# Layer 0 of a four-layer convolution stack: depthwise taps in halves three taps apart, with expansions on the free rows

## The chip, the cores and the metric

The kernel runs on one core of one Trainium2 chip. A time is the device time of one execution in microseconds. The core has TensorE (matrix products, "PE" in the profile, with its weight loads as "PEld"), VectorE (DVE), ScalarE (ACT), GpSimd (POOL) and SyncE (SP, which here only issues transfers). TensorE multiplies a stationary block of up to 128x128 with moving columns, and can be used as smaller tiles: a product with 32 rows and 32 columns takes one of 16 such tiles, one with 64 and 64 takes a quarter of the array. The rows of a tile are the partitions that its operands lie on, its columns are the partitions of the result in PSUM.

## The reference, cut to what matters

Four layers, each `x = x + layer(group_norm(x))`, on x of 4 images, 64 channels, 256x256, in fp32. Only layer 0 is touched:

```
def _L0_conv_ref(x, w_in, w_dw, fft_filter, w_out):
    x = einsum('bchw,oc->bohw', x, w_in)             # 64 -> 384 channels ("expansion")
    xf = rfft2(8x8 patches of x) * fft_filter        # a filter on each patch's spectrum
    x = irfft2(xf) put back together
    x = depthwise 3x3 convolution of x with w_dw, zero padding 1
    x1, x2 = split(x, 2, axis=1)                     # 192 and 192 channels
    x = gelu(x1) * x2
    return einsum('bchw,oc->bohw', x, w_out)         # 192 -> 64
def _gn(v, G=32, eps=1e-5):                          # mean and variance over 2 channels x H x W
    ...
```

Layer 1 is a dense 3x3 convolution, layer 2 a choice between two 1x1 convolutions by the local differences, layer 3 a product of the lowest Fourier modes.

## The kernel before, in words

An image is cut into 32 tiles of eight rows (NJ = 32), 128 tiles in all (NS). Layer 0 is a loop over steps t, with the parts of several tiles in one step: taps and gating of tile t, projection and residual of tile t - 1, expansion and inversion of tiles t + 1 and t + 2, and transposition and transformation of tile t + 2. The order of the instructions on TensorE, VectorE, ScalarE and SyncE is the order in which the program states them (`tc.manual_schedule`); semaphores make them wait for each other across engines. GpSimd runs in its own order.

For one tile: `normalize_x` (ScalarE) normalizes x. `transpose_x` (L358) makes eight 128x128 transpositions, so that the 64 pixels of a patch lie on partitions, two patches one above the other. `transform_x` (L366) multiplies with the patch transform in 64x64 tiles (L372). `expand` (L378, products at L385) multiplies spectra with w_in: 64 channels to 384, so each product has 64 rows, 64 columns of results and 384 moving elements. The four products of one call, two halves s of rows times two halves n of results, fill the array. VectorE then multiplies the two PSUM banks with the filter (L388) into `up`. `invert` (L415, products at L423, 64x64 with 64 moving elements) transforms back, and ScalarE copies the result into one of three planes y with a border (L430): plane 0 and 1 hold the first 128 of x1 and of x2, plane 2 the other 64 of both.

The depthwise convolution of planes 0 and 1 is done on TensorE, that of plane 2 on VectorE (`vector_tap`, nine instructions a tile, L488, the first on ScalarE, L486). On TensorE a tap is a product with a diagonal 32x32 block. `depthwise` (L442) goes through nine taps k, in each through four quarters q of the channels (rows of the array) and four chunks j of two image rows (columns of the array): 16 tiles of 32x32 with 512 moving elements (L450), into two pairs of PSUM banks, quarters 0 and 1 into the first, 2 and 3 into the second. A plane is done on all 16 tiles for nine taps; plane 0 gets a gelu on ScalarE (`gate_part`, L464), plane 1 is multiplied to it by VectorE (`value_part`, L470). `project` multiplies with w_out in 64x64 (L516) and 32x64 tiles (L525), `add_residual` and `finish` add x and take the statistics for layer 1. Transfers are tied to certain taps, so that they come at a set point of the step (`after`).

PSUM is four pairs of banks, given out in turn (`pair`). The statistics of image 0 come first: 32 parts of 8 rows, each loaded in two transfers to 64 partitions (L277), two VectorE instructions each (L269). A partition holds every second group of four rows of one channel. Those of the later images are taken in the steps, one part or two a step, `AHEAD` = 4 parts ahead (L570).

Of the kernel before, what the change touches and what calls it, by code (L numbers as in the profile page):

```python
# [17 lines left out]
C = 64  # L18
# [51 lines left out]
def _constants(H, W):  # L70
# [3 lines left out]
    avg = (grp[:, None] == grp[None, :]) / np.sum(grp == 0)  # L74
    half = np.arange(128) // C
# [9 lines left out]
        "c_ident": np.eye(128), "c_avg32": avg32, "c_sel32": sel32, "c_fdft": f_blk, "c_bdft": b_blk, "c_pick": pick, "c_avg": avg,  # L85
# [29 lines left out]
class _Net:  # L115
# [53 lines left out]
    def group_norm_parts(self, n, b, bst):  # L169


        nc, sp = self.nc, self.sp
# [4 lines left out]
        nc.tensor.matmul(ps[:, 0:1], self.avg, mv[:, 0:1], start=True, stop=True)  # L177
# [5 lines left out]
        nc.vector.scalar_tensor_tensor(q, d, d, mv[:, 1:2], ALU.mult, ALU.add)  # L183
        yield
        ps2 = self.small(f"gv{n}_{b}")
        nc.tensor.matmul(ps2[:, 0:1], self.avg, q, start=True, stop=True)
# [58 lines left out]
    def _layer0(self, ctx, dst):  # L245
# [3 lines left out]
        turn = count()  # L249

        def pair(name):

            return pp.tile([128, 2, 512], F32, tag=f"p{next(turn) % 4}", name=name)

        small = self.small = lambda name: pair(name)[:, 0, :]
# [9 lines left out]
        def input_stats(t, k, bst):  # L265
            tf = t.rearrange("p r w -> p (r w)")
            n = 4 * W // 512
            for i in range(n):
                nc.vector.bn_stats(bst[:, k * n + i, :], tf[:, i * 512 : (i + 1) * 512])  # L269

        new_bst0 = lambda b: self.sp.tile([128, NJ * 4 * W // 512, 6], F32, tag="bst0", name=f"bst0_{b}")
        with tc.tile_pool(name="l0i", bufs=12) as p_i:
            bst0 = new_bst0(0)
            for k in range(NJ):
                t = p_i.tile([128, 4, W], F32, tag="st", name=f"st_{k}")
                for s in range(2):
                    nc.sync.dma_start(t[halves[s]], src_t[0, :, k, s])  # L277
                input_stats(t, k, bst0)
            self.group_norm(0, 0, bst0)
# [78 lines left out]
        def transpose_x(t):  # L358
            xn = xns.pop(t)
            ps = pair(f"psT_{t}").rearrange("p z (k m) -> p (z k) m", m=128)  # L360
# [5 lines left out]
        def transform_x(t):  # L366
            x = xT.pop(t)
            ps = pair(f"psF_{t}").rearrange("p n (k m) -> p n k m", m=C)
# [9 lines left out]
        def expand(t, g, k):  # L378

            if k == 0:  # L380
                ups[t, g] = p_u.tile([128, 2, 4, 384], F32, tag="up", name=f"up_{t}_{g}")
            ps = pair(f"psu_{t}_{g}_{k}")
            for s in range(2):
                for n in range(2):
                    nc.tensor.matmul(  # L385
                        ps[halves[n], s, 0:384], xf[t][halves[s], n, 4 * g + k], win[halves[s]], start=True, stop=True
                    )
            nc.vector.tensor_mul(ups[t, g][:, :, k, :], ps[:, :, 0:384], flt.broadcast_to([128, 2, 384]))  # L388
# [26 lines left out]
        def invert(t, g, i):  # L415

            up = ups[t, g]
            ps = pair(f"psy_{t}_{g}_{i}").rearrange("p n (s r k w) -> p n s r k w", s=2, r=8, k=4)
# [23 lines left out]
        def depthwise(t, i, *transfers):  # L442


            d = [pair(f"psd_{t}_{i}_{m}").rearrange("p z (r w) -> p z r w", r=2) for m in range(2)]
            for k in range(9):
                dy, dx = divmod(k, 3)
                for q in range(4):
                    for j in chunks_of(t):
                        ins = nc.tensor.matmul(  # L450
                            d[q // 2][quarters[j], q % 2], diag[quarters[q], i, k, :],
                            rows_in(t, i, quarters[q], j, dy)[:, :, dx : dx + W],
                            start=(k == 0), stop=(k == 8), tile_position=(q * Q, j * Q),
                        )
                if k % 2 == 0 and k // 2 < len(transfers):
                    f, *args = transfers[k // 2]
                    f(*args, ins=ins)
            return d

        def gate_part(t, d):  # L460
            p = slice(0, Q * len(chunks_of(t)))
            h = ht[t] = p_h.tile([128, 4, 2, W], F32, tag="h", name=f"h_{t}")
            for m in range(2):
                nc.scalar.activation(h[p, 2 * m : 2 * m + 2], d[m][p], AF.Gelu)  # L464

        def value_part(t, d):
            p = slice(0, Q * len(chunks_of(t)))
            for m in range(2):
                hm = ht[t][p, 2 * m : 2 * m + 2]
                nc.vector.tensor_mul(hm, hm, d[m][p])  # L470
# [34 lines left out]
        def project(t, *groups):  # L505

            if 0 in groups:
                po[t] = [pair(f"pso_{t}_{m}") for m in range(1 if t == NS else 2)]
# [61 lines left out]
        AHEAD = 4  # L570

        def parts_of(t):
            if t < 0:
                return []
            more = [NJ + t // 6] if t < 6 * AHEAD and t % 6 == 4 else []
# [12 lines left out]
        def next_stats(t):  # L588
            for k in parts_of(t):
                b, j = place(k)  # L590
                if b not in bst0s:
                    bst0s[b], left[b] = new_bst0(b), NJ
                input_stats(st.pop(k), j, bst0s[b])
# [10 lines left out]
        with ordered:  # L604
# [3 lines left out]
            for t in range(2):  # L608
                normalize_x(t)
                transpose_x(t)  # L610
                transform_x(t)
            for k in range(4):
                expand(0, 0, k)
            new_y(0)
            for k in range(4):
                expand(0, 1, k)
                if k < 3:
                    invert(0, 0, k)
            for k in range(4):
                expand(1, 0, k)  # L620
                if k < 3:
                    invert(0, 1, k)
            vector_taps(0, 0)

            for t in range(NS + 2):

                if exists(t + 1):
                    new_y(t + 1)  # L630
                vector_gelu(t - 1, 0)
                normalize_x(t + 2)
                vector_taps(t, 1)
                vector_gate(t - 1, 0)
                vector_gelu(t - 1, 1)
                vector_taps(t, 2)
                vector_gate(t - 1, 1)
                vector_taps(t, 3, 4)
                if t <= NS:
                    loads = [(load_r, t, 0), (load_r, t, 1)]  # L640
                    if exists(t + 3):
                        loads += [(load_x, t + 3, 0), (load_x, t + 3, 1)]
                    gate_part(t, depthwise(t, 0, *loads))
                next_stats(t - 1)
                self.next_norms()

                if exists(t + 2):
                    transpose_x(t + 2)
                if exists(t + 1):
                    invert(t + 1, 0, 0)  # L650
                if t - 1 in rt:
                    project(t - 1, 0)
                if exists(t + 2):
                    transform_x(t + 2)
                if t - 1 in rt:
                    project(t - 1, 1, 2, 3)
                vector_taps(t, 5)
                if t - 1 in rt:
                    add_residual(t - 1)
                if exists(t + 1):  # L660
                    invert(t + 1, 0, 1)
                    expand(t + 1, 1, 0)
                    expand(t + 1, 1, 1)
                    invert(t + 1, 0, 2)
                    expand(t + 1, 1, 2)
                    expand(t + 1, 1, 3)
                if t - 1 in rt:
                    finish(t - 1)
                self.next_norms()

# [696 lines left out]
```

## Time and profile before

| | us |
|---|---|
| time, median of 3 runs (lowest to highest) | 7640.96 (7629.38 to 7649.89) |
| the profiled execution: time | 7615.35 |
| the profiled execution: span, first to last instruction | 7613.6 |
| PE busy | 7280.2 (96%) |
| DVE busy | 6592.5 (87%) |
| ACT busy | 3657.3 (48%) |
| L450, taps on TensorE | 2532.6 (73296 passes) |
| L488, taps on VectorE | 2390.8 |
| L385, expansions | 787.5 (8192 passes) |
| L423, inversions | 922.7 (49152 passes) |

"Busy" is the time in which at least one instruction of the group runs; matmuls overlap on TensorE, and their ends are modelled, so the starts carry more than the durations. A line of a group reads: line, engine, operation, result<-operands, tile of the array (rows*columns), shape of the moving operand, number. In an answer in order of time the first two numbers are the start and the length in us. An fp32 product appears as two matmul instructions, and each with its weight load. A row of a stretch gives the stretch, its length, and the busy time of PE, PEld, DVE, ACT and POOL with the number of instructions, then the clock granted to TensorE (1.00 is full speed), the busy share of the DMA engines and GB/s.

### The profile page before, as it was taken

The numbers are of one execution on the slowest core, as the hardware profiler recorded it, in microseconds if no ns is written. First come the engines' busy times: TensorE is split into PE (matmuls) and PEld (weight loads), VectorE is DVE, ScalarE is ACT, GpSimd is POOL, SyncE is SP. The second block draws the span as 40 slices with busy tenths as digits, with TensorE's granted clock in tenths as the row PEclk, the third lists the DMA queues.
The fourth block names the chain that finished last, engine by engine and source line by source line (L and its number), as shares of the span: only waits on it lengthen the run. The fifth ranks groups of instructions, "written<-read, shape, count | busy, mean of one in ns | idle before, by whom it ended". The sixth has DMA issues, their size and how long they took to land. (4 is left out here: it accounts for less than half of the span.)

```text
span 7613.6 us, 398948 instructions
## 1 busy us (share of the span) xinstructions
PE 7280.2 (96%) x189302; PEld 4316.7 (57%) x189302; DVE 6592.5 (87%) x5914; ACT 3657.3 (48%) x3917; POOL 658.8 (9%) x1435
## 2 busy tenths in 40 slices
PE   5999999999999999999999999899989999998797
PEld 3666666666666666666666666433324444443276
DVE  6999999999999999999999899899989888885345
ACT  2444444454544445444454454322238778774111
POOL 0000000000000000000000000001102222221011
PEclk9999999999999999999999999999999999999955
DMA  4222222222222222222111111478766766667789
GB/s 121 64 65 62 60 64 61 59 60 63 61 59 60 60 63 61 64 61 54 46 46 47 47 48 46 102 196 199 193 161 172 178 170 175 171 178 232 243 334 395
DMA packets 651427, 875.50 MB, mean 115 GB/s; under 512 B 44500, under 2 KB 470436, under 8 KB 647748
## 3 DMA queue, kind: packets, MB, share of 16 engines
q1 hardware_dynamic: 568772, 581.48, 29.0%
q0 software_dynamic: 81024, 268.50, 12.2%
q8 instruction: 1485, 24.33, 1.4%
q14 instruction: 146, 1.20, 0.1%
HBM read 581.37 MB, written 268.44 MB: 112 GB/s over the span
## 5 line engine op out<-in xcount | busy, mean ns | idle before, releaser
L450 PE MATMUL psd<-y,diag 32*32 32x512 f32 x73296 | 2532.6, 597 | 13.6 <-issue 13.0
L488 DVE SCALAR_TENSOR_TENSOR v<-y,sb_w_dw,v 128x2048 f32<-128x2048 f32 x1024 | 2390.8, 2335 | 110.7 <-ACT v L486 88.0
L450 PEld LDWEIGHTS psd<-y,diag 32*32 32x32 f32 x73296 | 1529.5, 103 | 851.3 <-issue 331.1
L430 ACT COPY y<-psy 128x512 f32<-128x512 f32 x1536 | 915.7, 660 | 1676.6 <-PE psy L423 1675.1
L388 DVE TENSOR_TENSOR up<-psu,flt 128x768 f32<-128x768 f32 x1024 | 932.5, 951 | 218.2 <-PE psu L385 217.7
L423 PEld LDWEIGHTS psy<-sb_c_bdft,up 64*64 64x64 f32 x49152 | 853.5, 135 | 345.0 <-issue 135.8
L423 PE MATMUL psy<-sb_c_bdft,up 64*64 64x64 f32 x49152 | 922.7, 221 | 27.3 <-issue 25.0
L385 PE MATMUL psu<-win,xf 64*64 64x384 f32 x8192 | 787.5, 489 | 22.2 <-DVE h L470 9.6
L988 DVE TENSOR_TENSOR q<-xn 128x2313 f32<-128x2313 f32 (+2 forms) x256 | 627.1, 2492 | 1.7 <-ACT xn L226 1.7
L1043 PE MATMUL one<-z,wp 32*32 32x512 f32 x16384 | 595.2, 598 | 19.6 <-issue 14.6
L989 ACT ACTIVATE q<-q 128x2313 f32<-128x2313 f32 (+2 forms) x256 | 528.9, 2086 | 33.4 <-DVE q L988 31.9
L226 ACT ACTIVATE xn<-x,nb,r 128x1024 f32<-128x1024 f32 (+3 forms) x272 | 488.0, 1798 | 42.2 <-DMA x<-x 32.3
L464 ACT ACTIVATE h<-psd 128x1024 f32<-128x1024 f32 x258 | 251.0, 1023 | 519.1 <-PE psd L450 518.8
L1043 PEld LDWEIGHTS one<-z,wp 32*32 32x32 f32 x16384 | 365.8, 103 | 227.9 <-issue 87.1
L1002 PE MATMUL div<-q,ones 64*32 64x512 f32 x8192 | 468.0, 597 | 12.3 <-ACT q L989 9.8
L395 POOL MEMSET y<- 128x22 f32 x384 | 51.9, 136 | 4228.6 <-ACT y L403 3219.8
L385 PEld LDWEIGHTS psu<-win,xf 64*64 64x64 f32 x8192 | 301.2, 134 | 191.5 <-issue 90.6
L1076 POOL DMA_DIRECT2D x<-r x512 | 273.6, 541 | 972.2 <-DVE r L1073 943.3
L797 PE MATMUL m<-t,wk 64*64 64x512 f32 x3072 | 352.7, 588 | 0.0
L797 PE MATMUL m<-t,wg 64*64 64x512 f32 x3072 | 343.6, 591 | 4.5 <-DVE wg L759 4.5
L1002 PEld LDWEIGHTS div<-q,ones 64*32 64x32 f32 x8192 | 156.1, 107 | 317.5 <-issue 246.0
L812 ACT COPY s<-m 128x1024 f32<-128x1024 f32 x64 | 64.8, 1013 | 558.9 <-PE m L797 548.7
(131 smaller groups left out, 7619.4 us busy)
## 6 DMA issues: line engine op xcount, KB each, us to landing
x<-x SPq DMA_DIRECT2D x240, 640.0 KB, 6.2
x<-x SPq DMA_DIRECT2D x122, 1024.0 KB, 11.6
st<-in_x_dram SPq DMA_DIRECT2D x256, 256.0 KB, 3.5
x<-in_x_dram SPq DMA_DIRECT2D x256, 256.0 KB, 3.8
x<-o POOLq DMA_DIRECT2D x128, 512.0 KB, 9.2
r<-x SPq DMA_DIRECT2D x512, 128.0 KB, 4.0
x<-r POOLq DMA_DIRECT2D x512, 128.0 KB, 3.9
out_dram<-x POOLq DMA_DIRECT2D x64, 1024.0 KB, 9.8
```

What stands on the lines that cost most here:

```text
L226: self.nc.scalar.activation(dst, src, AF.Identity, bias=self.nb[n][p0:p1, b : b + 1], scale=self.r[n][p0:p1, b : b + 1])
L385: nc.tensor.matmul(ps[halves[n], s, 0:384], xf[t][halves[s], n, 4 * g + k], win[halves[s]], start=True, stop=True)
L388: nc.vector.tensor_mul(ups[t, g][:, :, k, :], ps[:, :, 0:384], flt.broadcast_to([128, 2, 384]))
L423: nc.tensor.matmul(ps[halves[c], n, s, :, k, :], up[halves[n], s, k, i * 128 + c * C : i * 128 + (c + 1) * C], bdft[halves[n]], start=True ...
L430: nc.scalar.copy(yt[t][i][:, 3:11, w0 : w0 + 64].rearrange("p r (k n w) -> p n r k w", k=4, n=2), ps[:, :, s])
L450: ins = nc.tensor.matmul(d[q // 2][quarters[j], q % 2], diag[quarters[q], i, k, :], rows_in(t, i, quarters[q], j, dy)[:, :, dx : dx + W], ...
L488: nc.vector.scalar_tensor_tensor(v, s, wdw[:, 2, k : k + 1], v, ALU.mult, ALU.add)
L797: nc.tensor.matmul(rows2(m)[halves[j], s], gs[i][halves[s], dx, :], ts[n][halves[s], i, 2 * j : 2 * j + 2, dx : dx + W], start=(dx == 0), ...
L988: nc.vector.tensor_sub(d, p0, p1)
L989: nc.scalar.activation(d, d, AF.Square)
L1002: ins = nc.tensor.matmul(ps[quarters[j], h], ones[halves[h]], q[n, g, k][halves[h], r + 2 * j : r + 2 * j + 2, o : o + W], start=(m == 0), ...
L1043: ins = nc.tensor.matmul(rows2(ps[g])[quarters[j], k], w[quarters[i]], z[quarters[i], h, 2 * j + dy : 2 * j + dy + 2, dx : dx + W], tile_p ...
```

## The change

- The taps of a plane are no longer run on all 16 tiles for nine taps. The first half of the channels (quarters 0 and 1, rows 0 to 63 of the array) begins three taps before the second (quarters 2 and 3). So a plane has three stages: taps 0 to 2 of the first half; six rounds with tap k + 3 of the first and tap k of the second half; taps 6 to 8 of the second half. `taps` takes the place of `depthwise`.
- In the first and third stage half of the array's rows have no tap. Expansions are put there: `expand` now takes one half s of the rows and two columns k, and gives back its four products one by one (`give`) and the filter's instruction (`filtered`). After every third tap matmul one expansion product is issued, eight products in a stage of 24 tap matmuls.
- Two inversions stand between the rounds of plane 1's second stage. Gelu, value product, gates, transposition and the loads are restated around this, with PSUM pairs named instead of given out in turn. `transpose_x` runs for tile t + 3 at the end of the step.
- The statistics of later images run six parts ahead, and their two VectorE instructions stand in two places of a step.
- Image 0's statistics: a partition holds one half of a channel's rows in order, so a part is one transfer to 128 partitions. As this gives channel c on partitions 2c and 2c + 1, two new 128x128 constants average over groups and move the result to the usual places, with one more product and one more copy.

The diff, without the first tiles' lines ahead of the loop and the tags in unchanged functions; of the step's order the lines as they are after (the ones before are shown above):

```diff
--- before.py
+++ after.py
@@ constants
+    grpp = np.arange(128) // 2 // (C // GROUPS)
+    avgp = (grpp[:, None] == grpp[None, :]) / np.sum(grp == 0)
+    avgx = (grpp[:, None] == grp[None, :]) / np.sum(grp == 0)
...
@@ group_norm_parts
-    def group_norm_parts(self, n, b, bst):
+    def group_norm_parts(self, n, b, bst, avg=None):
+        same, moved = avg or (self.avg, self.avg)
-        nc.tensor.matmul(ps[:, 0:1], self.avg, mv[:, 0:1], start=True, stop=True)
+        nc.tensor.matmul(ps[:, 0:1], same, mv[:, 0:1], start=True, stop=True)
+        if moved is not same:
+            nc.tensor.matmul(ps[:, 1:2], moved, mv[:, 0:1], start=True, stop=True)
+        if moved is not same:
+            nc.vector.tensor_copy(gm, ps[:, 1:2])
-        nc.tensor.matmul(ps2[:, 0:1], self.avg, q, start=True, stop=True)
+        nc.tensor.matmul(ps2[:, 0:1], moved, q, start=True, stop=True)
...
@@ _layer0: PSUM pairs and image 0's statistics
-        turn = count()
-        def pair(name):
-            return pp.tile([128, 2, 512], F32, tag=f"p{next(turn) % 4}", name=name)
-        small = self.small = lambda name: pair(name)[:, 0, :]
+        def pair(tag, name):
+            return pp.tile([128, 2, 512], F32, tag=f"p{tag}", name=name)
+        small = self.small = lambda name: pair(2, name)[:, 0, :]
-        def input_stats(t, k, bst):
+        def input_stats(t, k, bst, *which):
-            for i in range(n):
+            for i in which or range(n):
-        with tc.tile_pool(name="l0i", bufs=12) as p_i:
+        with tc.tile_pool(name="l0i", bufs=12) as p_i, tc.tile_pool(name="l0a", bufs=1) as p_a:
+            flat = a["x"][0].rearrange("c (s h) w -> (c s) (h w)", s=2)
+            avgs = [self.load(name, p_a) for name in ("c_avgp", "c_avgx")]
-                for s in range(2):
-                    nc.sync.dma_start(t[halves[s]], src_t[0, :, k, s])
+                nc.sync.dma_start(t.rearrange("p r w -> p (r w)"), flat[:, 4 * W * k : 4 * W * (k + 1)])
-            self.group_norm(0, 0, bst0)
+            self.group_norm(0, 0, bst0, avgs)
...
@@ expand
-        def expand(t, g, k):
-            if k == 0:
+        def expand(t, g, s, k, tag):
+            if not exists(t):
+                return [], lambda: None
+            if (t, g) not in ups:
                 ups[t, g] = p_u.tile([128, 2, 4, 384], F32, tag="up", name=f"up_{t}_{g}")
-            ps = pair(f"psu_{t}_{g}_{k}")
-            for s in range(2):
-                for n in range(2):
-                    nc.tensor.matmul(
-                        ps[halves[n], s, 0:384], xf[t][halves[s], n, 4 * g + k], win[halves[s]], start=True, stop=True
-                    )
-            nc.vector.tensor_mul(ups[t, g][:, :, k, :], ps[:, :, 0:384], flt.broadcast_to([128, 2, 384]))
+            ps = pair(tag, f"psu_{t}_{g}_{s}_{k}")[:, :, 0:384]
+            def give(n, i):
+                nc.tensor.matmul(
+                    ps[halves[n], i], xf[t][halves[s], n, 4 * g + k + i], win[halves[s]], start=True, stop=True
+                )
+            def filtered():
+                nc.vector.tensor_mul(ups[t, g][:, s, k : k + 2, :], ps, flt.broadcast_to([128, 2, 384]))
+            return [(give, n, i) for i in range(2) for n in range(2)], filtered
...
@@ taps in place of depthwise
-        def depthwise(t, i, *transfers):
-            d = [pair(f"psd_{t}_{i}_{m}").rearrange("p z (r w) -> p z r w", r=2) for m in range(2)]
-            for k in range(9):
+        def bank_pair(t, i, m, tag):
+            return pair(tag, f"psd_{t}_{i}_{m}").rearrange("p z (r w) -> p z r w", r=2)
+        def taps(t, i, d, *parts, fill=()):
+            fill = list(fill)
+            work = [(m, k, q, j) for m, k in parts for q in (2 * m, 2 * m + 1) for j in chunks_of(t)]
+            for n, (m, k, q, j) in enumerate(work):
-                for q in range(4):
-                    for j in chunks_of(t):
-                        ins = nc.tensor.matmul(
-                            d[q // 2][quarters[j], q % 2], diag[quarters[q], i, k, :],
-                            rows_in(t, i, quarters[q], j, dy)[:, :, dx : dx + W],
-                            start=(k == 0), stop=(k == 8), tile_position=(q * Q, j * Q),
-                        )
-                if k % 2 == 0 and k // 2 < len(transfers):
-                    f, *args = transfers[k // 2]
-                    f(*args, ins=ins)
-            return d
-        def gate_part(t, d):
+                ins = nc.tensor.matmul(
+                    d[m][quarters[j], q % 2], diag[quarters[q], i, k, :],
+                    rows_in(t, i, quarters[q], j, dy)[:, :, dx : dx + W],
+                    start=(k == 0), stop=(k == 8), tile_position=(q * Q, j * Q),
+                )
+                if n % 3 == 2 and fill:
+                    f, *args = fill.pop(0)
+                    f(*args)
+            for f, *args in fill:
+                f(*args)
+            return ins
+        def gate_part(t, m, d):
-            h = ht[t] = p_h.tile([128, 4, 2, W], F32, tag="h", name=f"h_{t}")
-            for m in range(2):
-                nc.scalar.activation(h[p, 2 * m : 2 * m + 2], d[m][p], AF.Gelu)
-        def value_part(t, d):
+            if m == 0:
+                ht[t] = p_h.tile([128, 4, 2, W], F32, tag="h", name=f"h_{t}")
+            nc.scalar.activation(ht[t][p, 2 * m : 2 * m + 2], d[m][p], AF.Gelu)
+        def value_part(t, m, d):
-            for m in range(2):
-                hm = ht[t][p, 2 * m : 2 * m + 2]
-                nc.vector.tensor_mul(hm, hm, d[m][p])
+            hm = ht[t][p, 2 * m : 2 * m + 2]
+            nc.vector.tensor_mul(hm, hm, d[m][p])
...
@@ statistics ahead
-        AHEAD = 4
+        AHEAD = 6
-            more = [NJ + t // 6] if t < 6 * AHEAD and t % 6 == 4 else []
+            more = [NJ + t // 4] if t < 4 * AHEAD and t % 4 == 2 else []
-        def next_stats(t):
+        def next_stats(t, i):
-                    bst0s[b], left[b] = new_bst0(b), NJ
-                input_stats(st.pop(k), j, bst0s[b])
+                    bst0s[b], left[b] = new_bst0(b), 2 * NJ
+                input_stats(st[k] if i == 0 else st.pop(k), j, bst0s[b], i)
...
@@ the order of a step
             for t in range(NS + 2):
+                B2, C2, X, Y = 2, 3, t % 2, 1 - t % 2
+                vector_taps(t - 1, 8)
                 if exists(t + 1):
                     new_y(t + 1)
                 vector_gelu(t - 1, 0)
+                vector_gelu(t - 1, 1)
                 vector_taps(t, 1)
+                u = [expand(t + 1, 1, 1, 0, C2), expand(t + 1, 1, 1, 2, Y)]
+                if t <= NS:
+                    d = {0: bank_pair(t, 0, 0, B2)}
+                    ins = taps(t, 0, d, (0, 0), (0, 1), (0, 2), fill=u[0][0] + u[1][0])
+                    load_r(t, 0, ins=ins)
+                u[0][1]()
+                u[1][1]()
                 vector_gate(t - 1, 0)
+                vector_gate(t - 1, 1)
                 vector_taps(t, 2)
                 if t <= NS:
+                    d[1] = bank_pair(t, 0, 1, X)
+                    for k in range(6):
+                        ins = taps(t, 0, d, (0, k + 3), (1, k))
+                        if k == 1:
+                            load_r(t, 1, ins=ins)
+                        if k in (3, 5) and exists(t + 3):
+                            load_x(t + 3, k // 4, ins=ins)
+                    gate_part(t, 0, d)
+                u = [expand(t + 1, 1, 0, 0, C2), expand(t + 1, 1, 0, 2, Y)]
+                if t <= NS:
+                    taps(t, 0, d, (1, 6), (1, 7), (1, 8), fill=u[0][0] + u[1][0])
+                    gate_part(t, 1, d)
+                u[0][1]()
+                u[1][1]()
+                vector_taps(t, 3)
+                next_stats(t - 1, 0)
+                invert(t + 1, 0, 0, B2)
+                if t - 1 in rt:
+                    project(t - 1, 0, tags=(C2, X))
                 if exists(t + 2):
+                    transform_x(t + 2, Y)
                 if t - 1 in rt:
                     project(t - 1, 1, 2, 3)
                     add_residual(t - 1)
+                self.next_norms()
+                invert(t + 1, 0, 1, B2)
+                invert(t + 1, 0, 2, Y)
+                vector_taps(t, 4)
                 if t - 1 in rt:
                     finish(t - 1)
                 if exists(t + 1):
                     copy_y(t + 1)
+                u = [expand(t + 2, 0, 1, 0, C2), expand(t + 2, 0, 1, 2, X)]
+                if t + 1 == NS or place(t + 1)[1] == 0:
+                    last_y(t + 1)
+                if t <= NS:
+                    d = {0: bank_pair(t, 1, 0, B2)}
+                    ins = taps(t, 1, d, (0, 0), (0, 1), (0, 2), fill=u[0][0] + u[1][0])
+                    store(t - 1, 0, ins=ins)
+                else:
+                    store(t - 1, 0, 1)
+                u[0][1]()
+                u[1][1]()
+                vector_taps(t, 5)
+                next_stats(t - 1, 1)
                 vector_taps(t, 6, 7)
                 if t <= NS:
+                    d[1] = bank_pair(t, 1, 1, Y)
+                for k in range(6):
+                    if t <= NS:
+                        ins = taps(t, 1, d, (0, k + 3), (1, k))
+                    if k == 1 and t <= NS:
+                        store(t - 1, 1, ins=ins)
+                    if k == 2:
+                        invert(t + 1, 1, 2, X)
+                        vector_taps(t + 1, 0)
+                    if k in (3, 5) and t <= NS:
+                        load_stats(t, k // 4, ins=ins)
+                    if k == 4:
+                        invert(t + 1, 1, 0, C2)
+                normalize_x(t + 3)
+                if t <= NS:
+                    value_part(t, 0, d)
+                u = [expand(t + 2, 0, 0, 0, X), expand(t + 2, 0, 0, 2, C2)]
+                if t <= NS:
+                    taps(t, 1, d, (1, 6), (1, 7), (1, 8), fill=u[0][0] + u[1][0])
+                u[0][1]()
+                if t <= NS:
+                    value_part(t, 1, d)
+                u[1][1]()
+                if exists(t + 3):
+                    transpose_x(t + 3, X)
+                invert(t + 1, 1, 1, Y)
...
```

## The prediction

> **What bounds the kernel now.** I read the page's busy shares and slices first, to see which engine is full and where. Then the busy time by stretches and the instructions in order of time of one step of layer 0, and last single moments on TensorE.
>
> ```profile
> span 7613.6 us, 398948 instructions
> PE 7280.2 (96%) x189302; PEld 4316.7 (57%) x189302; DVE 6592.5 (87%) x5914; ACT 3657.3 (48%) x3917; POOL 658.8 (9%) x1435
> PE   5999999999999999999999999899989999998797
> ```
>
> Layer 0 runs from about 100 to 4870 us, over 60% of the span, and TensorE is full in it. One step, from one start of the depthwise taps to the same point a step later:
>
> ```profile
> 2005.81:2015.57 9.76, 9.76 (x291) 6.05 (x290) 9.48 (x5) 4.91 (x7) 0.00 (x0) 1.00 0.36 97
> 2015.57:2026.73 11.16, 11.04 (x376) 7.89 (x376) 9.45 (x10) 7.01 (x11) 0.00 (x0) 1.00 0.07 18
> 2026.73:2036.41 9.68, 9.68 (x291) 6.00 (x288) 9.61 (x10) 2.19 (x4) 0.81 (x2) 1.00 0.32 72
> 2036.41:2042.22 5.81, 5.81 (x229) 4.48 (x224) 5.59 (x6) 3.48 (x5) 0.96 (x3) 1.00 0.30 69
> ```
>
> The columns are length, then busy time of PE, weight loads, DVE, ACT and POOL, granted clock, DMA. Of 36.41 us TensorE is busy 36.27; VectorE 34.13, so it is close behind. A shorter step needs shorter work on TensorE. What its work costs, by moments on TensorE in order of time:
>
> ```profile
> 2026.32 0.49 PE L385 MATMUL psu<-win,xf 64*64 64x384 f32 x2
> 2026.73 0.66 PE L450 MATMUL psd<-y,diag 32*32 32x512 f32 x8
> ...
> 2035.78 0.70 PE L450 MATMUL psd<-y,diag 32*32 32x512 f32 x8
> ...
> 2035.89 0.59 PE L450 MATMUL psd<-y,diag 32*32 32x512 f32 x1
> 2036.41 0.27 PE L423 MATMUL psy<-sb_c_bdft,up 64*64 64x64 f32 x2
> ...
> 2037.39 1.55 PE L385 MATMUL psu<-win,xf 64*64 64x384 f32 x16
> 2038.69 0.26 PE L423 MATMUL psy<-sb_c_bdft,up 64*64 64x64 f32 x1
> ...
> 4856.02 7.93 PE L450 MATMUL psd<-l,diag 32*32 32x512 f32 x72
> ```
>
> Each fp32 matmul is two passes. What to see:
> - A full tap is 16 tiles of 32x32, 32 passes; nine take 9.75 us, 1.083 each.
> - Two expansions are 16 passes, four tiles at a time: 2037.39 to 2038.69, 1.30 us, so 0.325 a round.
> - With four tiles a tap pass costs 7.93 us / 18 = 0.44 us.
> - From the last 32x32 matmul (2035.89) to the first 64x64 one (2036.41) pass 0.52 us; from the last 64x64 expansion (2026.32) back to 32x32, 0.41 us. Between equal forms the next round comes after 0.44 and 0.325, so a change of form costs some 0.08 us over the streaming.
> - Who is waited for: the last eight tap matmuls, from 2035.78 on, are on rows 64 to 127 (L448 goes through the quarters in order). Between 2036.2 and 2036.42 no others are in flight any more, so those on rows 0 to 63 were through by 2036.2. The inversion's first matmul at 2036.41 reads rows 0 to 63 only (L421 to L425, n = 0 first). Had it waited for its own rows alone, it could have begun 0.2 us earlier or more. It began when the last matmul **on the other rows** was through. A 64x64 matmul doesn't run beside a 32x32 one here, even on free rows.
>
> **The change, part by part.**
>
> *Stages where half-height taps and expansions mix.* Four a step: 24 tap matmuls on two of the four row quarters, and after each third tap one expansion matmul on the other half, eight in all. The parts exist 127 times for the second halves of the next step's group 1 and 126 times for the step after's group 0, each in two stages: 2x127 + 2x126 = 506 stages.
> Before: 24 tap matmuls are 1.5 full taps, 1.625 us; eight expansion matmuls 1.30 us; together 2.92 us.
> After, if a change of form waits for everything in flight: three taps, on three different tiles, start together; second pass after 0.44; from its start to the expansion 0.52; its second pass 0.325 later; from that start to the next tap 0.41. Sum 1.70 us a group, eight groups 13.6 us. The rest of the array stands empty meanwhile. More per stage: 10.68 us; over 506 stages **5,404 us**.
> Bounds of a group: 1.52 if the 0.09 us at either switch goes (streaming alone: 0.44 + 0.43 + 0.65), and 1.96 if at each a 64-column weight load (0.13) lies bare as well. That gives 4,680 and 6,460 us. I take 1.70, as all its terms are measured switches between these very forms.
>
> [...]
>
> *Full taps in between*: six rounds in each half step, unchanged at 1.083 us. Two inversions now stand between these rounds: four more changes of form a step. A round's starts spread over 0.25 us, so 0.25 + 0.52 instead of 0.54 into the inversion and some 0.09 us on the way back: 0.3 us each, 0.6 a step, **about 75 us**.
>
> *VectorE, ScalarE*: the same instructions in another order. The filter (0.95 us, 1,024 of them) takes one half's two columns instead of two halves' one. All of VectorE's 34.1 us a step now have some 79 us to lie beside. Fixed bank pairs: a pair given back late would stop TensorE behind it (the transposition behind the last stage wants the pair of that stage's first expansion). Its filter can run during the stage's last four groups, 6.8 us. So 0; up to 1 us a step (127 us) if that cover is gone.
>
> *Queues*: the same transfers of x, r, statistics and results, each behind a tap matmul, in other places; SP spends 2.7 us on a pair and POOL 0.7 on a store, of a step twice as long. Statistics run two tiles further ahead and halve into two instructions' places: 0.
>
> *Start*: image 0 comes in 32 transfers to 128 partitions instead of 64 to 64. It is loaded at 251 GB/s until 73 us, with the DMA engines full, while VectorE's 64 statistics at 0.643 us need 41 us. Layer 3's loads to 128 partitions and stores, in 7310 to 7380, move 413 GB/s together. Bounds: 0 (if the rate stays) and 26 us; I take **20 us less**, by the nearer row. Two tiny matmuls, a copy and two 64 KB loads (0.45 us of issue each): 1 us more.
>
> *End*: six stages in the last two steps have no expansions, and run six passes at 0.44 = 2.64 us where 1.625 stood: 6 us more.
>
> *Sum* on the profiled execution: 7613.6 + 5404 + 75 - 20 + 1 + 6 = 13,080, and 2 us outside the span (its own time was 7615.35 for a span of 7613.6). The median of the runs, 7640.96, lies 26 us above that time: **13,100 us**. With the group's bounds 12,350 to 14,160.
>
> **Rivals.**
>
> *The clock falls too* (slower still). The granted clock goes by more than TensorE's busy time:
>
> ```profile
> 4857.00:4863.00 6.00, 6.00 (x64) 1.73 (x60) 3.89 (x8) 0.63 (x1) 1.37 (x2) 1.00 0.41 90
> 7310.00:7380.00 70.00, 64.23 (x357) 49.52 (x359) 44.73 (x72) 9.74 (x17) 12.04 (x16) 0.57 1.04 413
> ```
>
> In the first, one tile in each of the four row quarters streams and the clock is 1.00; in the second, layer 3's 32-row matmuls, often one row quarter at a time, are busy 92% of the time at 0.57. A mixed stage lies between: on average 1.5 row quarters for half of the time and two for 0.37 of it. [...]
>
> *The forms run side by side after all* (faster). For: only fully occupied arrays change form in this trace. Against: the 0.52 us above. Then a stage takes its longer half, six passes of 0.44 = 2.64 us against 2.92: 142 us less, and with 75 and the start about **7,560 us**, faster by 1.1%. It decides as soon as a stage takes less than 2.8 us, where the gain outweighs the inversions' switches.
>
> *TensorE gathers equal forms past each other*: at 2025.2 matmuls of two lines on 64x64 tiles start mingled. Were all taps of a stage done first, then its expansions: 2.64 + 2.6 (eight rounds on half the array) + 0.2 for two switches = 5.4 us, 2.5 us more: 8,950 us.
>
> **How the numbers follow.** Everything drained at full clock 0.56, drained with the clock down in part or whole 0.31, side by side 0.08, gathered 0.05. The range, 12,300 to 18,700, takes in the first with its bounds (12,350 to 14,160 alone) and most of the second. Faster by over 0.3%, which is about what a measurement here can tell from none, 0.08; slower 0.91; same 0.01.
>
> **What would show it.** Right: layer 0 ends near 10,350 us; groups of three tap matmuls and one expansion matmul repeat every 1.7 us; VectorE's share falls to about 50%, TensorE's stays over 90%. Clock rival: PEclk below 9 through the first 30 slices. Wrong: expansions starting within 0.1 us of a tap on the other rows, a stage of 2.6 to 3 us. The start shows by itself: statistics done before 60 us, or still at 73.

## The result and the profile after

The changed kernel takes **17,875.19 us** (median of 4 runs, 17,862.30 to 17,935.84), beside 7,645.43 us of the kernel before (4 runs, 7,629.38 to 7,656.83): a ratio of **2.340, 95% interval 2.333 to 2.347**. It lies in the predicted range, but not at the predicted 13,100 us: the time is nearest to the first rival, in which the clock falls too and for which the range reaches to 18,700 us. The profiled execution took 17,935.84 us.

The page of the changed kernel: the span, the busy shares, two rows of slices, and the two groups that the change mixes (L471 are the taps, L398 the expansions).

```profile
span 17934.0 us, 398633 instructions
PE 17606.6 (98%) x189304; PEld 5571.4 (31%) x189304; DVE 6632.0 (37%) x5915; ACT 3694.7 (21%) x3917; POOL 657.0 (4%) x1435
PE   8999999999999999999999999999999999999988
PEclk7666666666666666666666666666666667999996
L471 PE MATMUL psd<-y,diag 32*32 32x512 f32 x73296 | 8492.3, 798 | 30.7 <-issue 30.1
L398 PE MATMUL psu<-win,xf 64*64 64x384 f32 x8192 | 5209.0, 733 | 0.0
```

The numbers of passes are those of before (73,296 and 8,192); their busy times have gone from 2,532.6 to 8,492.3 us and from 787.5 to 5,209.0. TensorE is busy 98% and never waits for long, and yet its granted clock is near 0.66 as long as layer 0 lasts, from the second slice to the thirty-fourth. VectorE's work is the same 6,600 us, now 37% of the span.

TensorE in order of time, in the first and in the third stage of plane 1 of one step (start, length in us). One stage is eight times six tap passes and two expansion passes:

```profile
5042.99 1.05 PE L471 MATMUL psd<-y,diag 32*32 32x512 f32 x6 [0.41 <-issue]
5043.97 0.86 PE L398 MATMUL psu<-win,xf 64*64 64x384 f32 x2
5044.76 1.05 PE L471 MATMUL psd<-y,diag 32*32 32x512 f32 x6
...
5074.79 0.86 PE L398 MATMUL psu<-win,xf 64*64 64x384 f32 x2
5075.58 1.05 PE L471 MATMUL psd<-y,diag 32*32 32x512 f32 x6
5076.56 0.86 PE L398 MATMUL psu<-win,xf 64*64 64x384 f32 x2
...
5080.89 1.26 PE L471 MATMUL psd<-y,diag 32*32 32x512 f32 x6
5082.08 1.54 PE L398 MATMUL psu<-win,xf 64*64 64x384 f32 x2
5083.55 1.92 PE L471 MATMUL psd<-y,diag 32*32 32x512 f32 x6
5085.40 1.54 PE L398 MATMUL psu<-win,xf 64*64 64x384 f32 x2
```

Two things are to be read here. First, the two kinds strictly take turns: three taps, then one expansion, then three taps, although they use different rows. Second, a group lasts 1.77 us at the beginning of a stage (5074.79 to 5076.56), and 3.32 from the middle of it on (5082.08 to 5085.40): everything takes nearly twice as long from some 8 us after the stage's beginning.

Stretches of the same kernel (length, then busy time and number of instructions of PE, PEld, DVE, ACT and POOL, granted clock, DMA share, GB/s): the start, a long piece of layer 0, and within one step four stretches in a row: most of plane 1's first stage; its end and the full rounds; plane 1's third stage; and an inversion with plane 0's first stage of the next step.

```profile
10.00:40.00 30.00, 0.00 (x0) 0.00 (x0) 30.00 (x48) 0.00 (x0) 0.00 (x0) 1.00 1.03 410
...
1000.00:4000.00 3000.00, 2983.32 (x29725) 859.45 (x29725) 882.08 (x727) 466.79 (x581) 48.10 (x133) 0.66 0.08 20
...
5042.99:5057.80 14.81, 14.81 (x55) 2.42 (x55) 3.41 (x6) 3.14 (x5) 0.13 (x1) 0.77 0.00 1
5057.80:5074.79 16.99, 16.99 (x339) 6.26 (x336) 9.22 (x6) 5.13 (x6) 1.37 (x2) 0.70 0.23 49
5074.79:5095.41 20.62, 20.62 (x69) 4.60 (x67) 4.40 (x5) 0.39 (x1) 0.13 (x1) 0.67 0.05 14
5095.41:5123.88 28.47, 28.47 (x129) 5.56 (x128) 4.64 (x3) 3.25 (x4) 0.13 (x1) 0.50 0.00 1
```

A step takes 118.6 us on average where it took 36.4. TensorE is busy in every microsecond of these four stretches, at a clock between 0.77 and 0.50. What a share of busy time can't show, the clock column does. (The clock's records hold only 1.00 and 0.50, each for a multiple of 3.41 us, so a value in between is a mean over the stretch. They agree with the spacing of the matmuls: in the first of these stretches the groups slow down some 8 us in, and 8 us at 1.00 with 6.8 us at 0.50 make the 0.77 of the row.)

Over all 506 stages, by the spacing of the expansions: eight groups at full clock would be 14.2 us, and a stage takes 21.7 on average. None keeps full clock to its end. Plane 0's third stage and both of plane 1 nearly always begin at full clock and fall later (20.8 to 21.0 us a stage; of all stages that begin so, half fall within 6.8 us, most after 3.5 to 9); plane 0's first stage, with only a transposition and an inversion between it and the mixed stage before, begins at half clock four times in ten and takes 24.4. That is 7.6 us a stage on top of the 14.2. The full rounds behind a stage begin at half clock too.

### The profile page after: what moved, and what is told of

Same layout as the page of the kernel before. It is cut to its first block, busy times and chain, and to the rows that moved or that the text cites. A ratio compares the mean times of both kernels' runs of the same rounds, so it can differ in the third digit from the quotient of the medians.

```text
span 17934.0 us, 398633 instructions
## 1 busy us (share of the span) xinstructions
PE 17606.6 (98%) x189304; PEld 5571.4 (31%) x189304; DVE 6632.0 (37%) x5915; ACT 3694.7 (21%) x3917; POOL 657.0 (4%) x1435
## 5 line engine op out<-in xcount | busy, mean ns | idle before, releaser
L471 PE MATMUL psd<-y,diag 32*32 32x512 f32 x73296 | 8492.3, 798 | 30.7 <-issue 30.1
L398 PE MATMUL psu<-win,xf 64*64 64x384 f32 x8192 | 5209.0, 733 | 0.0
L471 PEld LDWEIGHTS psd<-y,diag 32*32 32x32 f32 x73296 | 1691.6, 118 | 4569.6 <-issue 4395.8
L398 PEld LDWEIGHTS psu<-win,xf 64*64 64x64 f32 x8192 | 1006.5, 173 | 5337.7 <-issue 4822.9
L442 PE MATMUL psy<-sb_c_bdft,up 64*64 64x64 f32 x49152 | 1177.5, 251 | 56.1 <-issue 38.8
L442 PEld LDWEIGHTS psy<-sb_c_bdft,up 64*64 64x64 f32 x49152 | 1067.7, 160 | 476.4 <-issue 393.6
L492 DVE TENSOR_TENSOR h<-h,psd 128x1024 f32<-128x1024 f32 x258 | 314.8, 1221 | 1674.0 <-PE psd L471 1662.1
L518 ACT ACTIVATE g<-v 64x1024 f32<-64x1024 f32 x257 | 270.8, 1054 | 3080.9 <-DVE v L525 3046.3
L374 ACT COPY xT<-psT 128x1024 f32<-128x1024 f32 x128 | 129.5, 1012 | 2665.3 <-PE psT L372 2665.3
L525 DVE TENSOR_TENSOR v<-g,v 64x1024 f32<-64x1024 f32 x257 | 313.4, 1219 | 151.3 <-ACT g L518 147.3
```

What stands on the lines that cost most here:

```text
L398: nc.tensor.matmul(ps[halves[n], i], xf[t][halves[s], n, 4 * g + k + i], win[halves[s]], start=True, stop=True)
L442: nc.tensor.matmul(ps[halves[c], n, s, :, k, :], up[halves[n], s, k, i * 128 + c * C : i * 128 + (c + 1) * C], bdft[halves[n]], start=True ...
L471: ins = nc.tensor.matmul(d[m][quarters[j], q % 2], diag[quarters[q], i, k, :], rows_in(t, i, quarters[q], j, dy)[:, :, dx : dx + W], start ...
```

## The experiments

Two causes are multiplied here, the changes of form and the clock. Theories: (a) a change of form waits until everything in flight is through, whatever rows it is on, so time goes by the number of changes; (b) the clock falls because of what streams during a mixed stage. For (b) the candidates were the number of form changes, the number of tiles in use, and the number of row quarters in use. Unless said otherwise each edit is to the changed kernel. Beside the first four of these runs the kernel before took 7,623 us (median of 3 runs), beside the last two 7,638 (14 runs).

### Half as many changes of form

```diff
-                if n % 3 == 2 and fill:
-                    f, *args = fill.pop(0)
-                    f(*args)
+                if n % 6 == 5:
+                    for f, *args in fill[:2]:
+                        f(*args)
+                    del fill[:2]
```

> The changed kernel with six taps and then two expansion products in turn, instead of three and one: half as many changes of form, the same products. Theory (every change between 32x32 and 64x64 empties TensorE): a group of six taps and two products, which use different tiles, lasts as long as a group of three and one did (1.77 us in the changed kernel at full clock), four groups a stage, 7.1 us instead of 14.2; the array is twice as full, so the clock stays up: 7,645 + 506 x (7.1 - 2.92) + about 60 = 9,800 us. Rival (the cost lies in each inserted product, for instance in its weight load, or in a wait for a bank): as many as before, so at least 13,000 us.

Measured: 9,930.83 us, ratio to before 1.302 (1.297 to 1.307). TensorE in order of time, and a long piece of layer 0:

```profile
3022.14 0.86 PE L398 MATMUL psu<-win,xf 64*64 64x384 f32 x4
3022.93 1.07 PE L471 MATMUL psd<-y,diag 32*32 32x512 f32 x12
3023.93 0.86 PE L398 MATMUL psu<-win,xf 64*64 64x384 f32 x4
...
1000.00:4000.00 3000.00, 2953.27 (x63724) 1229.48 (x63707) 1881.57 (x1562) 1002.63 (x1246) 106.61 (x296) 0.98 0.17 41
```

A group now holds twice the work, 12 tap passes and four expansion passes, and lasts 1.79 us from expansion to expansion, as long as the group of half that work did. So the time goes by the changes of form, not by the matmuls: on different tiles of the same form, twice as many run beside each other for nothing. And with twice as many tiles in use the clock stays up (0.98 from 1000 to 4000 us). This run changed both the changes of form and the occupancy, so it does not tell the candidates for the clock apart.

### No mixing: all taps of a stage, then its expansions

```diff
-                if n % 3 == 2 and fill:
-                    f, *args = fill.pop(0)
-                    f(*args)
```

> The changed kernel with all eight expansion products of a stage after its 24 taps: two changes of form a stage instead of sixteen. Theory: six passes on half the array at 0.44 = 2.64 us, eight rounds on the other half at 0.325 = 2.6 us, two changes 0.2 us: 5.4 us a stage, clock up: 7,645 + 506 x 2.5 + about 60 = 8,970 us. Rival (half-height stages are slow in themselves, by the order or by the bank pairs): over 10,000 us.

Measured: 9,015.70 us, ratio 1.182 (1.177 to 1.187). TensorE in order of time, the mixed stages from plane 1's first on, and the next step's plane 0:

```profile
3007.66 3.27 PE L471 MATMUL psd<-y,diag 32*32 32x512 f32 x48 [0.42 <-issue]
3010.86 2.80 PE L398 MATMUL psu<-win,xf 64*64 64x384 f32 x16
3013.59 3.41 PE L471 MATMUL psd<-y,diag 32*32 32x512 f32 x96
...
3025.26 2.80 PE L398 MATMUL psu<-win,xf 64*64 64x384 f32 x16
...
3030.10 2.80 PE L471 MATMUL psd<-y,diag 32*32 32x512 f32 x48
3032.84 2.80 PE L398 MATMUL psu<-win,xf 64*64 64x384 f32 x16
3035.57 9.22 PE L471 MATMUL psd<-y,diag 32*32 32x512 f32 x240
3044.72 1.51 PE L398 MATMUL psu<-win,xf 64*64 64x384 f32 x8
```

A stage takes 5.47 us (3030.10 to 3035.57), and its two changes of form are all that is left of 16. Still each kind fills only half of the array, so the stage takes nearly twice the 2.92 us of before. 506 stages by 2.55 us are 1,290 of the 1,392 us by which this kernel is slower than the one before. Beside it the changed kernel's 14.16 us at full clock, with the same products and eight changes there and back instead of one, give a price: 8.69 us for seven, 1.24 us each.

Two more terms of the prediction can be read here. Plane 1's 240 tap passes after the first expansions, with two inversions between them, last 11.67 us (3013.59 to 3025.26); the same 240 passes of plane 0, without inversions, last 9.15 (3035.57 to 3044.72). So the two inversions cost 2.52 us there. In the kernel before, an inversion ahead of an expansion of the same form took 0.98 us (2036.41 to 2037.39). The rest, 0.56 us a step, is what the prediction put at 0.6. And TensorE stands still for 0.42 us ahead of plane 1's first tap here, which the prediction put at nothing.

### Expansions as 32x32 tiles

```diff
-                nc.tensor.matmul(
-                    ps[halves[n], i], xf[t][halves[s], n, 4 * g + k + i], win[halves[s]], start=True, stop=True
-                )
+                for q in range(2):
+                    for c in range(2):
+                        p, o = quarters[2 * s + q], quarters[2 * n + c]
+                        nc.tensor.matmul(
+                            ps[o, q], xf[t][p, n, 4 * g + k + i, c * Q : (c + 1) * Q], win[p],
+                            start=True, stop=True, tile_position=((2 * s + q) * Q, (2 * n + c) * Q),
+                        )
```

> The changed kernel with every expansion product of 64x64 replaced by four of 32x32, each on a quarter of the rows and of the columns, so that taps and expansions have one form; the order stays mixed as it was. It leaves out the sum of the two halves of the 64 channels, and one of every two columns is overwritten, so the times are of the same streaming but not of the same result. Theory (form alone decides): they run side by side; a stage has 112 passes at 0.034 us, the spacing of the taps, 3.8 us: 7,645 + 506 x 0.9 + 60 = 8,160 us, clock up. Rival (any product between the taps stops them, whatever its form): 13,000 us or more.

Measured: 8,294.71 us, ratio 1.087 (1.083 to 1.092), clock 1.00 from 1000 to 4000 us. TensorE in order of time (the taps are L475 here, the expansions L401):

```profile
3007.89 0.62 PE L475 MATMUL psd<-y,diag 32*32 32x512 f32 x3 [0.42 <-issue]
3007.91 0.53 PE L401 MATMUL psu<-win,xf 32*32 32x384 f32 x4
3007.94 0.63 PE L475 MATMUL psd<-y,diag 32*32 32x512 f32 x3
3007.97 0.53 PE L401 MATMUL psu<-win,xf 32*32 32x384 f32 x4
...
3011.44 3.60 PE L475 MATMUL psd<-y,diag 32*32 32x512 f32 x91
```

Taps and expansions now start 0.02 to 0.03 us after each other. On the same rows and in the same places of the program they mingle as soon as they have one form. This is what shows that the form, and nothing else in the order of the work, made them take turns. The stage has 112 passes instead of 64 and takes 3.55 us (3007.89 to 3011.44), one pass each 0.032 us; so even this, which leaves out a sum that the computation needs, does not get down to the 2.92 us of before.

### What the clock goes by: the order over row quarters

These two runs change only the order of the 24 taps of a mixed stage: the same tiles, the same groups of three and one, the same number of changes of form. In the changed kernel the taps go by tap, then quarter, then chunk, so that a group of three lies on one row quarter or on two. In the first run here a group lies on two quarters whenever it can, in the second the quarter changes only once in a stage.

```diff
+            if fill:
+                work = [(m, k, q, j) for m, k in parts for j in chunks_of(t) for q in (2 * m, 2 * m + 1)]
```

> The changed kernel with the taps of a mixed stage in another order: the two row quarters in turn, so that each group of three taps has tiles in both, where it was one quarter or two (1.5 on average). Number of products, of changes of form and of used tiles are the same. Theory (the clock goes by the row quarters that stream: 1.5/4 of half the time and 2/4 of a third is 0.37 of the time before, 0.43 now, and it falls below a threshold between 0.31 and 0.43): the clock stays up, a stage lasts 8 x 1.77 = 14.2 us: 7,645 + 506 x 11.3 + 60 = 13,400 us. Rival (the clock goes by the used share of the 16 tiles, 0.18 in both): 17,900 us within 1%.

Measured: 13,562.41 us, ratio 1.778 (1.765 to 1.791).

```diff
+            if fill:
+                work = [(m, k, q, j) for q in (2 * parts[0][0], 2 * parts[0][0] + 1) for m, k in parts for j in chunks_of(t)]
```

> The changed kernel with the taps of a mixed stage in the order of the row quarters, 12 on the first and then 12 on the second, so that each group of three taps uses one row quarter only; the rest is the same. Theory (row quarters): 0.31 of the time instead of 0.37, the clock falls as early or earlier: 17,900 to 18,600 us. Rival (used share of the tiles): 17,900 us within 1%. If this differs from the changed kernel and the other order doesn't, the threshold lies elsewhere than I think.

Measured: 18,725.18 us, ratio 2.452 (2.446 to 2.459). The same stretch of the two kernels, first with the quarters taking turns, then with one quarter at a time:

```profile
1000.00:4000.00 3000.00, 2972.22 (x41549) 979.60 (x41550) 1230.90 (x1016) 654.30 (x812) 68.83 (x190) 0.96 0.11 27
```

```profile
1000.00:4000.00 3000.00, 2983.57 (x28212) 830.18 (x28210) 838.87 (x688) 444.56 (x552) 45.11 (x124) 0.63 0.08 19
```

| order of the taps in a mixed stage | time | row quarters streaming, mean share | clock, 1000 to 4000 us | PE busy there | mean stage |
|---|---|---|---|---|---|
| one quarter at a time | 18,725 | 0.32 | 0.63 | 99.5% | 23.6 |
| as in the changed kernel | 17,875 | 0.38 | 0.66 | 99.4% | 21.7 |
| two quarters in each group | 13,562 | 0.44 | 0.96 | 99.1% | 14.5 |

The third column is worked out from a group of 1.77 us at full clock: its expansion streams on two of the four quarters for 0.374 + 0.325 us, which gives 0.20; its taps stream for two times 0.43 us, on one quarter in all groups (0.12 more), in half of them (0.18), or on two in all (0.24). It is a measure that I chose, not one that the profile gives; the expectations had it 0.01 lower. The order of 24 matmuls alone moves 5,163 us, while busy time, tiles in use and changes of form stay what they were. That settles it between the candidates: the clock goes with the row quarters that are streaming, and not with TensorE's busy time, the number of tiles in use or the changes of form. One more thing differs in the first run: a group of three taps lies on two column quarters, where it lay on three. Columns alone don't explain the clock: in the second run a group lies on three as before and the clock falls further, and with six taps a group, above, it lies on all four, and on two row quarters, with the clock at 0.98. The second run is slightly above its expected 17,900 to 18,600.

In the changed kernel the granted clock was 0.66 from 1000 to 4000 us with TensorE busy 99.4% of that stretch, and no idle stretch of TensorE in layer 0 was longer than 1.8 us.

What stays open is the exact measure and its threshold. Between 0.38 and 0.44 by my measure the clock tips over; but with two quarters in each group, 12 in 100 of plane 1's first stages, and none of the three other kinds, still fall to half. TensorE's short idle stretch, which only these stages have just ahead of them, doesn't explain it: it stands ahead of 7 of the 15 that fall and of 64 of the 111 that don't.

### Image 0's statistics alone

The kernel before, with nothing but the new order of image 0's statistics:

```diff
+            flat = a["x"][0].rearrange("c (s h) w -> (c s) (h w)", s=2)
+            avgs = [self.load(name, p_a) for name in ("c_avgp", "c_avgx")]
...
-                for s in range(2):
-                    nc.sync.dma_start(t[halves[s]], src_t[0, :, k, s])
+                nc.sync.dma_start(t.rearrange("p r w -> p (r w)"), flat[:, 4 * W * k : 4 * W * (k + 1)])
...
-            self.group_norm(0, 0, bst0)
+            self.group_norm(0, 0, bst0, avgs)
```

> The kernel before with image 0's statistics alone taken as in the change: one transfer of a part to 128 partitions, two constants and two small instructions more. Theory: the statistics end at 49 us instead of 73 (as in the changed kernel), and all that follows is 24 us earlier: 7,621 us, a ratio of 0.9969. Rival (the steps of layer 0 wait for something else at the start): no difference.

Measured: 7,610.06 us (median of 9 runs, 7,601.20 to 7,616.38) beside 7,637.83 (14 runs), ratio 0.9963 (0.9951 to 0.9974): 28 us less. This is the fastest kernel of the study. The stretch at the start of the kernel before, and at the start of this one:

```profile
10.00:70.00 60.00, 0.00 (x0) 0.00 (x0) 37.30 (x58) 0.00 (x0) 0.00 (x0) 1.00 1.03 252
...
10.00:50.00 40.00, 0.00 (x0) 0.00 (x0) 39.96 (x63) 0.00 (x0) 0.00 (x0) 1.00 0.93 372
```

VectorE has no gap any more: 63 instructions in 40 us, one every 0.634 us, where it had 58 in 60 us before. The transfers bring 372 GB/s in this stretch (410 from 10 to 40 us of the changed kernel) instead of 252. The first tap comes at 92.8 us instead of 117.3. So VectorE is now the limit of this part, and the loads are not.

## Why the prediction was right and wrong

**A change of form waits for everything in flight: right.** It was the decisive step, and the 0.52 us at one switch of the kernel before was enough to see it. The group had been put at 1.70 us (bounds 1.52 to 1.96) and takes 1.77. One part is the second pass of a lone expansion, 0.374 us after the first (43.97 and 44.344 of a group) where I had taken the 0.325 of a round of four; the other is the first part of the group, 0.98 where 0.44 + 0.52 = 0.96 stood. Over 8 groups and 506 stages that is 283 us more: 14.16 - 2.92 = 11.24 us a stage, 5,687 us for 5,404. (Two slips in the prediction's own figures change nothing: the step's busy time of TensorE adds up to 36.29 us, not 36.27, and with the bound of 4,680 us the sum gives some 12,380, not 12,350.)

**The clock stays up: wrong, and this is the step that failed.** I gave it 0.56 and the rival 0.31. The four row quarters with one tile each at 1.00 and layer 3's 32-row matmuls at 0.57 were the right rows to lay side by side, and they say that row quarters matter. I let the mixed stage, in between, go to the better end without a reason in the trace; the runs above show that it lies just below the point where it tips, at 0.38 where 0.44 would mostly have done. That the measured time lies in the range at all is luck in this sense: the range had been drawn so as to take in most of the rival, and the account to which I gave 0.56 ends at 14,160 us.

**The size of the rival.** The 18,700 us at the end of the range stand for some 11 us more a stage than the 13,100 at full clock, a term of mine that no run shows. On average there are 7.6 us more in a stage, because a stage that starts at full clock mostly keeps it for 3.5 to 9 us (median 6.8, and 8 in the two stages shown). For all of it: the profiled execution took 17,936 us. The terms without the clock are 7,615 + 5,687 + 71 (inversions) + 24 (idle) - 12 (start) + 6 (end, as predicted) = 13,391. What is left, 4,545 us, is 9.0 us a stage: 7.6 in it and 1.4 in what follows. The same comes out in another way. By the clock's records 10,008 us of layer 0 are spent at half clock. A group takes 1.77 instead of 3.32 us at full clock, so 0.467 of this would have been saved, 4,670 us, which gives about 13,270. And the kernel with two quarters in each group, where the clock mostly stays up, takes 13,562 us. So the mixed stages at full clock cost about 5,690 us, and the clock about 4,600. Of the 5,690, the kernel without mixing still pays 1,290, mostly for the half-empty array; the other 4,400 are the changes of form.

**Inversions between rounds**: 0.56 us a step instead of 0.6, 71 us for 75: right. **Waits**: put at 0, up to 127 us; the idle time of TensorE at taps, inversions and expansions rose from 63.1 to 86.8 us, some 24, 17 of it at the taps, where some 0.4 us stand ahead of plane 1's first one in 73 of 126 steps, and nothing there waited for a pair of banks. **VectorE and ScalarE** as the cover of their own work: right, VectorE's 37% leaves room everywhere.

**Start**: 20 us less predicted (0 to 26). The statistics are through at 49.1 us instead of 73.5, 24 us earlier; alone this is worth 28 us. Of these only 12 arrive at the first tap of the changed kernel (105.3 us instead of 117.3). There the first expansions go to two tiles at a time on half the rows (their 96 passes take 20.4 us, with the statistics alone changed 10.9), and three tiles are transposed first: the prediction had overlooked the lines ahead of the loop. As the end of the statistics went to VectorE's own pace, "by the nearer row" (413 GB/s) was the right choice.

**What I said would show it.** The two kinds never started within 0.1 us of each other (0.41 us was the least); PE stayed over 90%; statistics were done before 60 us. Layer 0 did not end near 10,350 us but near 15,180, and VectorE's share is 37% and not 50%: these two went with the clock, which was below 9 in slices 1 to 34, as the rival wanted.

The two other rivals are out. Side by side (7,560 us) needed the forms to overlap; in 4,048 switches no expansion started less than 0.51 us after the last tap's start, and in 3,795 back no tap less than 0.41 us after the last expansion's. One form, at four products for one, did not pay either: a stage takes 3.55 us and not 2.64. Gathered (8,950 us): the machine does not reorder the two kinds here, but the program can, and written out this way it took 9,016 us. The price of 5.4 us a stage was right (5.47).

Taps and expansions on different rows overlapped in these runs only where both were 32x32 tiles: there they start 0.02 to 0.03 us after each other.

## What to carry to other kernels

Before two kinds of matmul are put on free parts of TensorE's array, look whether they have the same tile form; if not, count the changes of form and multiply by what the runs show for one of them (here 1.24 us for a change there and back around a few matmuls), and group equal forms as far as the program allows. Free rows are no spare time: a stage whose two kinds each fill half of the rows, one after the other, took 5.47 us here for work that took 2.92 on all of them, and stages that stream on too few row quarters can lose clock besides (0.66 from 1000 to 4000 us, with TensorE busy 99%). When a sum has a factor of two on one term (a clock that may hold or fall), make the runs or find the row that settles this before polishing the other terms.

## What the runs showed of the hardware that was not expected

- The order of the same 24 small matmuls over row quarters decides on the clock: 0.63, 0.66 or 0.96 in the same stretch, at 99% busy each time. The changed kernel's clock records know only full and half clock, each for a multiple of 3.41 us.
- A stage on too few rows, begun at full clock, mostly keeps it for 3.5 to 9 us (some 8 in the two shown) and never gets it back before its end; the dense rounds after it are at full clock again by the first inversion, about 5 us on (5062.58 to 5068.27 for 96 passes that take 3.33 us at full clock, and the next 64 at full speed again).
- The second pass of a lone 64x64 matmul with 384 fp32 elements begins 0.374 us after the first; with four tiles in turn it is 0.325.
- Loads of image 0 to 128 partitions ran at 410 GB/s, to 64 partitions in two transfers at 252, both with the DMA engines at a busy share of 1.03.
